# Normalized rows turned by full transposes, v's products regrouped, and identity products in planned TensorE pauses, in a window-attention and Fourier-mixer kernel

## The chip, the core and the metric

The program runs on one core of one Trainium2 chip. The metric is device time in microseconds (us) of one execution, from the first to the last instruction, with what lies around them. The core's engines are TensorE (PE in the profile, its weight loads PEld), VectorE (DVE), ScalarE (ACT), GpSimd (POOL) and SyncE (SP), which issues the DMAs here. All data is 32-bit float but the small bias product (bfloat16).

## What is computed

The input x is [8 images, 192 channels, 64 rows, 64 columns]. Two layers follow each other:

```python
# layer 0: window attention with a top-16 mask, then an MLP
shortcut = layer_norm(tokens(x))                       # over the 192 channels
q, k, v = split(windows_8x8(shortcut) @ qkv_w.T + qkv_b)   # 6 heads of 32
attn = (l2n(q) @ l2n(k).T) * temperature
attn = softmax(where(attn >= 16th_largest(attn), attn, -100) + rpb)
x2 = shortcut + unwindow((attn @ v) @ proj_w.T + proj_b)
x2 = x2 + gelu(layer_norm(x2) @ fc1_w.T + fc1_b) @ fc2_w.T + fc2_b
# layer 1: a Fourier mixer, then an MLP
y = x2 + real(ifft2(mlp_2_16_2(fft2(layer_norm(x2)))))
out = y + gelu(layer_norm(y) @ mlp1_w.T + mlp1_b) @ mlp2_w.T + mlp2_b
```

## The kernel before

**Tiling.** An image is cut into 8 bands of 512 tokens (8 rows of 64 columns, so 8 windows), and its channels into 12 groups of 16 for the Fourier part. The tasks of one image are: `front` once per band (load, transpose to tokens, norm, transpose back to channels, q, k and v), `attention` twice per band (one half of the windows each), `back` once per band (projection and MLP of layer 0), `forward`, `pointwise` (twice) and `inverse` once per channel group (the Fourier mixer; it needs all 8 bands of the image), and `leave` once per band (MLP of layer 1 and the way out; it needs all 12 groups).

**The order of work.** Nothing is ordered by hand. Every task is a Python generator that yields `op(engine, weight, mode, get, put, after)` before it emits its instructions. `issue` is a planner that runs when the program is built: it keeps a clock for each engine, in units of about 10 ns, and always emits the step that can begin first, with ties broken by due times. A step's weight is its foreseen duration; a step of TensorE costs 20 units more when its mode (the way that it tiles the array: "full", "row64", "row32", "col32", "col64", "s", "v") differs from that of the step before. `get` and `put` take and return buffers: `ps` is one of 4 PSUM tiles of [128, 2, 512], `xn` the one buffer of normalized channels, `qk` the one of q and k, `vv` one of 2 for v. A step on `EITHER` goes to ScalarE or VectorE, whichever is foreseen to end first. The engines run in the order in which the planner emits, each waiting on semaphores for its data.

**Streams.** The tasks stand in streams, each with a width (how many of its tasks are open at once) and due times in images: `front` has width 2, `attention` 4, `back` 2, `forward` 1, `pointwise` 2, `inverse` 1, `leave` 2. Image b's Fourier groups are due from b + 1.055 on, so they run beside the bands of image b + 1; in the first image there is attention and the first MLP alone.

**The part of `front` that is changed.** The normalized tokens of a band lie in `xt` (tokens on partitions, 2 x 384 columns). They go back to channels in the PSUM tile `pc`, named lc in the profile: channels 0 to 127 fill 512 columns by four PE transposes (L539, in the helper `to_channels`); channels 128 to 191 go into 256 more columns, with the window's two column halves on partitions 0 to 63 and 64 to 127. That second part is a step of its own in mode "col64": eight fp32 products of 64 columns with pieces of the identity (L680), recorded as 16 matmuls. A copy (L814, two instructions, one step on `EITHER`) reorders both parts into `xn`. Then TensorE makes the rows of q and k for the two halves of the windows (`pq`: part a over 128 channels in mode "full", L749; part b over 64 channels in "row64", L763, with the bias product L768), and of v (`pv`: part a L786, part b L798). The order of these steps is qk a(0), qk b(0), qk b(1), qk a(1), v a, v b. L809 and L810 scale `xt` on GpSimd afterwards.

Six full transposes of the same form, L539 and L544 together, are used for the MLPs' inputs already (lc_b and lc_d in the profile).

Of the kernel before, what the change touches and what calls it, by code (L numbers as in the profile page):

```python
# [15 lines left out]
C = 192  # L16
# [6 lines left out]
DFF = 768  # L23
U = 33
EPS = 1e-5
NEG = -100.0


# [1 line left out]
    return engine, weight, mode, get.split(), (put + " " + put_too).split(), after, done  # L30


def issue(streams, units):

    change = {"pe": 20, "act": 130, "dve": 0, "pool": 0}
    clock = {e: 0 for e in change}
    mode = {e: None for e in change}  # L40
    units = {name: [0] * n for name, n in units.items()}
    events = {}
    live = []

    def advance(task, value):
        try:
            found = task["gen"].send(value)
            while not isinstance(found, tuple):

                new = dict(task, gen=found, queue=None)  # L50
                live.append(new)
                advance(new, None)
                found = task["gen"].send(None)
            task["op"] = found
        except StopIteration:
            live.remove(task)
            if task["queue"] is not None:
                start(task["queue"])

    def start(queue):  # L60
        if queue[0]:
            gen, place = queue[0].pop(0)
            task = {"gen": gen, "queue": queue, "urgency": 360 * place, "last": (None, 0)}
            queue[1] += 1
            task["order"] = (queue[1], len(live), place)
            live.append(task)
            advance(task, None)

    for tasks, width in streams:
        queue = [list(tasks), 0]  # L70
        for _ in range(width):
            start(queue)
    while live:
        best, ready = {}, {}
        for task in live:
            engines, weights, kind, get, put, after, done = task["op"]
            if isinstance(engines, str):
                engines, weights = (engines,), (weights,)
            free = 0
            deps = [task["last"]] if after is None else after  # L80
            deps = [d if d[0] is None or d[0] in change else events.get(d) for d in deps]
            if any(d is None for d in deps):
                continue
            short = False
            for name in set(get):
                n = get.count(name)
                if len(units[name]) < n:
                    short = True
                    break
                free = max(free, sorted(units[name])[n - 1])  # L90
            if short:
                continue
            found = []
            for engine, weight in zip(engines, weights):
                begin = max(clock[engine], free)
                for source, end in deps:
                    if source is not None and source != engine:
                        end += 30 if source == "pe" else 15
                    begin = max(begin, end)
                new = kind and mode[engine] and kind != mode[engine]  # L100
                cost = change[engine] if new else 0
                found.append((begin + cost + weight, engine, begin, cost, task, weight))

            _, engine, *rest = min(found, key=lambda f: f[0] + 40 * (f[1] == "dve"))
            ready.setdefault(engine, []).append((engine, *rest))
        for engine, found in ready.items():
            first = min(begin + cost for _, begin, cost, *_ in found) + 15
            best[engine] = min(
                [
                    (  # L110
                        begin + cost + task["urgency"] - 100 * ("ps" in task["op"][4]),
                        task["order"],
                        f,
                    )
                    for f in found
                    for _, begin, cost, task, _ in [f]
                    if begin <= first
                ],
                key=lambda v: v[:2],
            )  # L120
        choice = min(best.values(), key=lambda v: (v[2][1], v[:2]))[2]
        engine, begin, change_cost, task, weight = choice
        _, _, kind, get, put, after, done = task["op"]
        for name in get:
            units[name].remove(min(units[name]))
        end = begin + change_cost + weight
        clock[engine] = end
        if kind:
            mode[engine] = kind
        for name in put:  # L130
            units[name].append(end + 15)
        task["last"] = (engine, end)
        if done:
            events[done] = (engine, end)
        advance(task, (engine, end))
# [3 lines left out]
def kernel(  # L139
# [25 lines left out]
        tc.tile_pool(name="psp", bufs=4, space=bass.MemoryType.PSUM)  # L165
    )

    def psum(name):
        return psp.tile([128, 2, 512], FP, tag="ps", name=name)


    ATT_BUFS, H_BUFS, XT_BUFS = 5, 7, 4
# [473 lines left out]
    def front(b, i):  # L646
# [22 lines left out]
        last = yield from normalized(xt, pair, pair, mv, f"a{nm}")  # L669
        xts[b, i] = xt  # L670

        yield op("pe", 44, "full", get="ps xn", after=last)
        pc = flat(f"lc_{nm}")
        to_channels(pc, pair, xt, parts=(0,))
        moved = yield op("pe", 43, "col64")
        side = ident.rearrange("p (e h s) -> p h e s", e=2, h=2)
        for t, j in PAIRS:
            q = 2 * t + j
            for h in range(2):
                nc.tensor.matmul(  # L680
                    pc[64 * h : 64 * h + 64, BAND + q * 64 : BAND + (q + 1) * 64],
                    xt[:, j, CA + 64 * t : CA + 64 * t + 64],
                    side[:, h],
                    start=True,
                    stop=True,
                )
        normal = yield op(EITHER, (102, 115), put="ps")
        xn = strip("xn", 1, f"xn_{nm}")
        for cols, n in ((slice(0, BAND), 8), (slice(BAND, ROW), 4)):
            copy(  # L690
                normal,
                xn[:, cols].rearrange("p (w r k) -> p r w k", w=n, k=8),
                pc[:, cols].rearrange("p (r w k) -> p r w k", w=n, k=8),
            )

        more = b == 0 and i % 2 == 1 and i < 8
        places = ("qk", "h") if more else ("qk", "vv")
# [69 lines left out]
                rows = slice(64 * t, 64 * t + 64)  # L767
                nc.tensor.matmul(pq[:, t, : 2 * C], ones3[rows], qb3[rows], start=False, **flags)  # L768

        yield op("pe", 128, "full", get=f"ps {places[0]} {places[1]}", after=[normal, "qkv"])  # L770
        pq = psum(f"pq_{nm}_0")
        qk_a(pq, 0, True)
        last = yield op("pe", 80, "row64")
# [2 lines left out]
        yield op("pe", 80, "row64", get="ps", after=[])  # L776
        pq = psum(f"pq_{nm}_1")
        qk_b(pq, 1, True)
        yield op("pe", 128, "full")
        qk_a(pq, 1, False)  # L780
        yield squares(1, pq)
        yield op("pe", 128, "full", get="ps", after=[])
        pv = psum(f"pv_{nm}")
        for p in range(2):
            for t in range(2):
                nc.tensor.matmul(  # L786
                    pv[:, t, p * C : (p + 1) * C],
                    xn[:, (2 * t + p) * 128 : (2 * t + p + 1) * 128],
                    wqkv[0][:, 2 * C :],
                    start=(p == 0),  # L790
                    stop=False,
                    skip_group_check=True,
                )
        whole = yield op("pe", 64, "row64", put="xn")
        for p in range(2):
            for t in range(2):
                rows = slice(64 * t, 64 * t + 64)
                nc.tensor.matmul(  # L798
                    pv[:, t, p * C : (p + 1) * C],
                    xn[rows, BAND + p * 128 : BAND + (p + 1) * 128],  # L800
                    wqkv[1][rows, 2 * C :],
                    start=False,
                    stop=True,
                    skip_group_check=True,
                )
        yield values(whole)

        yield op("pool", 368, after=[normal, "rows"], done=("xt", b, i))
        nc.gpsimd.tensor_tensor(xt, xt, gain1, ALU.mult)  # L809
        nc.gpsimd.tensor_tensor(xt, xt, bias1, ALU.add)  # L810

# [374 lines left out]
    def leave(b, j):  # L1186
# [40 lines left out]
    bands = [(b, i) for b in range(B) for i in range(NB)]  # L1227
    at_band = lambda b, i, late: b + i / NB + late
    groups = [(b, n) for b in range(B) for n in range(NG)]
    at_group = lambda b, n: b + 1.055 + .755 * n / NG  # L1230
    layer1 = (vec(N2G), vec(N2B))
    streams = [
        ([(setup_qkv(), -1)], 1),
# [2 lines left out]
        ([(setup_mlp(0, lambda: (wfc1, wfc2), vec(G2), vec(B2), ["rows", (None, 3000)]), -0.5)], 1),  # L1236
        ([(setup_layer1(), 0.2)], 1),
        ([(setup_mlp(1, lambda: wmlp, *layer1, ["layer1", ("att", 0, 5, 1)]), 0.2)], 1),
        ([(front(b, i), at_band(b, i, -.12)) for b, i in bands], 2),
        ([(attention(b, i, hb), at_band(b, i, -.07)) for b, i in bands for hb in range(2)], 4),  # L1240
        ([(back(b, i), at_band(b, i, .2)) for b, i in bands], 2),
        ([(forward(b, n), at_group(b, n)) for b, n in groups], 1),
        ([(pointwise(b, n, k), at_group(b, n)) for b, n in groups for k in range(2)], 2),
        ([(inverse(b, n), at_group(b, n)) for b, n in groups], 1),
        ([(leave(b, j), b + 1.69 + .55 * j / NB) for b, j in bands], 2),
    ]
    with tc.manual_schedule():
        issue(streams, units)


# [78 lines left out]
```

## Time and profile before

| | us |
|---|---|
| median of 3 runs | 4892.78 (4886.49 to 4913.86) |
| the profiled execution | 4900.75 |
| its span, first to last instruction | 4899.0 |
| VectorE busy | 2855.5 |
| ScalarE busy | 2681.7 |
| PE weight loads busy | 3656.9 |
| mean granted TensorE clock | 0.973 of full speed |

A busy time is the time in which at least one instruction of the engine is in flight. Matmuls are pipelined: each is recorded with its whole latency, so the mean duration of one is longer than the time by which it moves the next one back. What a step takes of TensorE's time is therefore read from starts: from its first start to that of the next step, less the idle time that the timeline gives between them.

### The profile page before, as it was taken

What the parts mean: (1) busy time and instruction counts of PE and PEld (TensorE: products, weight loads), DVE (VectorE), ACT (ScalarE), POOL (GpSimd) and SP (SyncE); (2) the same over time, 40 slices, a digit from 0 to 9 for tenths busy, and PEclk for the clock granted to TensorE, in tenths of its full rate; (3) what the DMA queues carried; (4) which work ended last, traced back from release to release, by engine and by line L of the source; (5) the groups of instructions that cost most, each with busy time, mean ns of one, the idle gap of its engine ahead of it and who ended that gap; (6) DMA issues with size and microseconds to landing.
All of it is one profiled execution on the core that took longest, in us unless ns stands there. A gap on an engine that the chain in (4) does not pass through costs nothing.

```text
span 4899.0 us, 145236 instructions
## 1 busy us (share of the span) xinstructions
PE 4604.9 (94%) x62794; PEld 3656.9 (75%) x62794; DVE 2855.5 (58%) x10312; ACT 2681.7 (55%) x3887; POOL 2366.7 (48%) x2195
## 2 busy tenths in 40 slices
PE   6778999999999999999999999999999999999989
PEld 4556777887778877887777877788777876778768
DVE  6877656457755467565765656665667456662111
ACT  3445656456654566544665456644666355653553
POOL 5567645355554455453655445545465354641200
PEclk7878999999999999999999999999999999999999
DMA  2000000000000000000000000000000000000000
GB/s 49 17 8 11 6 9 9 17 18 12 9 5 21 18 9 9 8 24 15 5 9 15 17 15 9 9 15 20 9 9 9 21 18 9 2 5 17 8 4 24
DMA packets 54105, 63.97 MB, mean 13 GB/s; under 512 B 17583, under 2 KB 36218, under 8 KB 53466
## 3 DMA queue, kind: packets, MB, share of 16 engines
q1 hardware_dynamic: 53454, 54.68, 3.9%
q8 instruction: 494, 8.09, 0.7%
q14 instruction: 145, 1.19, 0.1%
q10 hardware_dynamic: 12, 0.00, 0.0%
HBM read 29.29 MB, written 25.17 MB: 11 GB/s over the span
## 4 chain that ended last, share of the span: by engine, by line
PE 75%; POOL 10%; DVE 7%; ACT 5%; issue 2%; DMA 0%; SPq 0%; ACTq 0%; POOLq 0%; DVEq 0%
PE mo_d L633 10%; PE mo_b L633 9%; PE fh L1090 7%; PE mh_d L587 6%; PE mh_b L587 6%; PE fo L1117 6%; POOL nrm L733 4%; PE mh_d L600 3%; PE mh_b L600 3%; PE pq L749 3%; ACT fh L1073 2%; PE fa L1020 2%; PE fy L1165 2%; PE fb L1138 2%; PE pq L763 2%
## 5 line engine op out<-in xcount | busy, mean ns | idle before, releaser
L1073 ACT ACTIVATE fh<-fh,ab 128x1024 f32<-128x1024 f32 x768 | 815.8, 1112 | 315.9 <-PE fh L1090 313.1
L877 POOL TENSOR_TENSOR s<-s,top 128x768 f32<-128x768 f32 x128 | 191.7, 1498 | 1022.0 <-DVE s L874 613.8
L733 POOL TENSOR_TENSOR nrm<-nrm,mhalf 128x24 f32<-128x24 f32 x128 | 547.3, 4276 | 10.7
L633 PE MATMUL mo_b<-wfc,h_b 128*128 128x192 f32 x3072 | 515.9, 327 | 1.0 <-ACT fh L1073 0.7
L633 PE MATMUL mo_d<-wmlp,h_d 128*128 128x192 f32 x3072 | 513.7, 327 | 0.1
L633 PEld LDWEIGHTS mo_b<-wfc,h_b 128*128 128x128 f32 x3072 | 498.3, 190 | 9.3 <-issue 5.3
L633 PEld LDWEIGHTS mo_d<-wmlp,h_d 128*128 128x128 f32 x3072 | 498.9, 190 | 6.5 <-issue 3.0
L1090 PE MATMUL fh<-fz,w1p 32*128 32x248 f32 (+1 forms) x6144 | 458.8, 402 | 18.9 <-ACT fh L1073 9.6
L1090 PEld LDWEIGHTS fh<-fz,w1p 32*128 32x128 f32 x6144 | 289.8, 184 | 140.5 <-issue 77.2
L1117 PE MATMUL fo<-fh,w2p 128*32 128x264 f32 (+1 forms) x6144 | 382.6, 386 | 4.6 <-ACT fh L1073 3.9
L587 PE MATMUL mh_b<-hn_b,wfc_a 128*128 128x256 f32 x1536 | 379.9, 396 | 5.7 <-ACT hn_b L814 3.7
L869 DVE MAX8 top<-s 128x8 f32<-128x64 f32 x1536 | 349.8, 228 | 53.3
L587 PE MATMUL mh_d<-hn_d,wmlp_a 128*128 128x256 f32 x1536 | 367.4, 387 | 4.8 <-ACT hn_d L814 2.3
L571 ACT ACTIVATE h_d<-mh_d,fcb 128x512 f32<-128x512 f32 x384 | 240.6, 686 | 191.3 <-PE mh_d L600 149.1
L587 PEld LDWEIGHTS mh_b<-hn_b,wfc_a 128*128 128x128 f32 x1536 | 286.7, 194 | 75.3 <-issue 25.3
L867 DVE MAX8 top<-s 128x8 f32<-128x64 f32 x1536 | 319.9, 208 | 38.9 <-ACT s L814 38.6
L587 PEld LDWEIGHTS mh_d<-hn_d,wmlp_a 128*128 128x128 f32 x1536 | 285.0, 191 | 64.0 <-issue 20.9
L868 DVE MATCH_REPLACE8 s<-top,s 128x64 f32<-128x64 f32 x1536 | 320.4, 209 | 0.0
L887 POOL TENSOR_TENSOR s<-s,rsum 128x768 f32<-128x768 f32 x128 | 191.8, 1500 | 255.8 <-DVE top L867 136.8
L1117 PEld LDWEIGHTS fo<-fh,w2p 128*32 128x32 f32 x6144 | 185.5, 110 | 155.6 <-issue 32.0
L571 ACT ACTIVATE h_b<-mh_b,fcb 128x512 f32<-128x512 f32 x384 | 241.3, 688 | 108.4 <-PE mh_b L600 73.9
L1203 DVE TENSOR_TENSOR zt<-mo_d,xy 128x768 f32<-128x768 f32 x64 | 61.2, 957 | 389.2 <-PE mo_d L633 331.4
(218 smaller groups left out, 8960.7 us busy)
## 6 DMA issues: line engine op xcount, KB each, us to landing
xin<-in_x SPq DMA_DIRECT2D x64, 256.0 KB
out<-z SPq DMA_DIRECT2D x64, 256.0 KB
xin<-in_x SPq DMA_DIRECT2D x128, 64.0 KB
out<-z SPq DMA_DIRECT2D x128, 64.0 KB
wfc<-in_wfc SPq DMA_DIRECT2D x1, 576.0 KB
wmlp<-in_wmlp SPq DMA_DIRECT2D x1, 576.0 KB
wfc_a<-in_wfc SPq DMA_DIRECT2D x1, 384.0 KB
wfc_b<-in_wfc SPq DMA_DIRECT2D x2, 192.0 KB
```

Of the source, the lines that this page charges most:

```text
L571: nc.scalar.activation(h[:, k].rearrange("p (t n) -> p t n", t=2), ph[:, :, k * HALF : (k + 1) * HALF], AF.Gelu, bias=fc1_bias[:, 2 * fp + ...
L587: nc.tensor.matmul(ph[:, t, k * HALF : (k + 1) * HALF], w1[0][:, f], hn[:, t * HALF : (t + 1) * HALF], start=(first and k == 0), stop=not ...
L600: nc.tensor.matmul(ph[:, t, k * HALF : (k + 1) * HALF], w1[1][rows, f], hn[rows, BAND:ROW], start=(first and k == 0), stop=not first, skip ...
L633: nc.tensor.matmul(acc[:, j, t * C : (t + 1) * C], hs[f // 2][:, f % 2, q * 128 : (q + 1) * 128], w2[:, f, ORDER[t]], start=(f == 0 and t ...
L733: nc.gpsimd.tensor_tensor(nf, nf, mhalf[:, :24], ALU.pow)
L867: nc.vector.max(first, of)
L868: nc.vector.match_replace(s2, first, of, -3.0e38)
L869: nc.vector.max(top[:, k // 4, k % 4, 8:16], s2)
L887: nc.gpsimd.tensor_tensor(s, s, row(rsum), ALU.mult)
L1073: nc.scalar.activation(hs[hf, k], ph, AF.Gelu, bias=ab[:, 0:1])
L1090: nc.tensor.matmul(phs[k // 2][:, k % 2, cols], w1p[i][rows, hf].rearrange("p h v -> p (h v)"), fz[rows, :] if rhs is None else zu[rows, : ...
L1117: nc.tensor.matmul(po[rows, :] if i == 0 else pou[rows, :, 1 : U - 1], w2p[i][:, hf].rearrange("p a v -> p (a v)"), hs[hf, k // 2][:, k % ...
```

## The change

Four things are changed.

1. Channels 128 to 191 go back by two full transposes (L544's form) in the same step as the other four. The quarters of the 256 columns that stand on the wrong partitions are moved by the copy: it is now two steps, one instruction for the first 512 columns, and four instructions of 64 partitions x 128 elements for the rest, each step on ScalarE or VectorE.
2. v's part b comes right after qk b(1), in the run of "row64" steps; v's part a comes last.
3. The planner notes, for each TensorE step, the pause that it foresees before it and after its PSUM tiles are free. Where this is 60 units or more, `psum` emits one product of the identity with itself (128x128x128, fp32) per 22 units of pause into the new PSUM tile, ahead of the step's own products.
4. Streams: `front` is 1 wide and `attention` 3, and several due times move.

```diff
+FILL = 60
...
-def issue(streams, units):
+def issue(streams, units, lull):
...
+        if engine == "pe":
+            tiles = get.count("ps")
+            given = sorted(units["ps"])[tiles - 1] if tiles else begin
+            lull["pe"] = begin - max(clock["pe"], given)
...
+    lull = {"pe": 0}
+
     def psum(name):
-        return psp.tile([128, 2, 512], FP, tag="ps", name=name)
+        tile_ = psp.tile([128, 2, 512], FP, tag="ps", name=name)
+        pause, lull["pe"] = lull["pe"], 0
+        if pause >= FILL:
+            for _ in range(int(pause / 22)):
+                nc.tensor.matmul(tile_[:, 0, 0:128], ident, ident, start=True, stop=True)
+        return tile_
...
-        yield op("pe", 44, "full", get="ps xn", after=last)
+        moved = yield op("pe", 66, "full", get="ps xn", after=last)
         pc = flat(f"lc_{nm}")
-        to_channels(pc, pair, xt, parts=(0,))
-        moved = yield op("pe", 43, "col64")
-        side = ident.rearrange("p (e h s) -> p h e s", e=2, h=2)
-        for t, j in PAIRS:
-            q = 2 * t + j
+        to_channels(pc, pair, xt)
+        xn = strip("xn", 1, f"xn_{nm}")
+        normal = []
+        for part in range(2):
+            weights = (100, 100) if part else (62, 67)
+            normal.append((yield op(EITHER, weights, put="ps" if part else "", after=[moved])))
+            if part == 0:
+                copy(
+                    normal[0],
+                    xn[:, :BAND].rearrange("p (w r k) -> p r w k", w=8, k=8),
+                    pc[:, :BAND].rearrange("p (r w k) -> p r w k", w=8, k=8),
+                )
+                continue
             for h in range(2):
-                nc.tensor.matmul(
-                    pc[64 * h : 64 * h + 64, BAND + q * 64 : BAND + (q + 1) * 64],
-                    xt[:, j, CA + 64 * t : CA + 64 * t + 64],
-                    side[:, h],
-                    start=True,
-                    stop=True,
-                )
-        normal = yield op(EITHER, (102, 115), put="ps")
...
+                for t in range(2):
+                    copy(
+                        normal[1],
+                        xn[64 * h : 64 * h + 64, BAND:].rearrange("p (w r k) -> p r w k", w=4, k=8)[
+                            :, 4 * t : 4 * t + 4
+                        ],
+                        pc[64 * t : 64 * t + 64, BAND:ROW].rearrange(
+                            "p (r w k) -> p r w k", w=8, k=8
+                        )[:, :, 4 * h : 4 * h + 4],
+                    )
...
         pq = psum(f"pq_{nm}_1")
         qk_b(pq, 1, True)
-        yield op("pe", 128, "full")
-        qk_a(pq, 1, False)
-        yield squares(1, pq)
-        yield op("pe", 128, "full", get="ps", after=[])
+        yield op("pe", 64, "row64", get="ps", after=[])
         pv = psum(f"pv_{nm}")
...
+        yield op("pe", 128, "full", after=[])
+        qk_a(pq, 1, False)
+        yield squares(1, pq)
+        whole = yield op("pe", 128, "full", put="xn", after=[])
...
-    at_group = lambda b, n: b + 1.055 + .755 * n / NG
+    at_group = lambda b, n: b + 1.025 + .725 * n / NG
...
-        ([(front(b, i), at_band(b, i, -.12)) for b, i in bands], 2),
-        ([(attention(b, i, hb), at_band(b, i, -.07)) for b, i in bands for hb in range(2)], 4),
-        ([(back(b, i), at_band(b, i, .2)) for b, i in bands], 2),
+        ([(front(b, i), at_band(b, i, -.12)) for b, i in bands], 1),
+        ([(attention(b, i, hb), at_band(b, i, -.085)) for b, i in bands for hb in range(2)], 3),
+        ([(back(b, i), at_band(b, i, .215)) for b, i in bands], 2),
...
-        ([(leave(b, j), b + 1.69 + .55 * j / NB) for b, j in bands], 2),
+        ([(leave(b, j), b + 1.72 + .52 * j / NB) for b, j in bands], 2),
```

More of the change, by code (lines that the diff above doesn't have):

```diff
@@ L670, in front @@
         xts[b, i] = xt
-        yield op("pe", 44, "full", get="ps xn", after=last)
+        moved = yield op("pe", 66, "full", get="ps xn", after=last)
         pc = flat(f"lc_{nm}")
-        to_channels(pc, pair, xt, parts=(0,))
-        moved = yield op("pe", 43, "col64")
-        side = ident.rearrange("p (e h s) -> p h e s", e=2, h=2)
-        for t, j in PAIRS:
-            q = 2 * t + j
-            for h in range(2):
-                nc.tensor.matmul(
-                    pc[64 * h : 64 * h + 64, BAND + q * 64 : BAND + (q + 1) * 64],
-                    xt[:, j, CA + 64 * t : CA + 64 * t + 64],
-                    side[:, h],
-                    start=True,
-                    stop=True,
-                )
-        normal = yield op(EITHER, (102, 115), put="ps")
[L688 to L694, printed above, removed]
+        to_channels(pc, pair, xt)
[11 more added lines that the diff above has]
+                continue
+            for h in range(2):
+                for t in range(2):
[8 more added lines that the diff above has]
+                    )
         more = b == 0 and i % 2 == 1 and i < 8
@@ L768, in qk_b @@
                 nc.tensor.matmul(pq[:, t, : 2 * C], ones3[rows], qb3[rows], start=False, **flags)
-        yield op("pe", 128, "full", get=f"ps {places[0]} {places[1]}", after=[normal, "qkv"])
+        yield op("pe", 128, "full", get=f"ps {places[0]} {places[1]}", after=[*normal, "qkv"])
         pq = psum(f"pq_{nm}_0")
@@ L778, in front @@
         qk_b(pq, 1, True)
-        yield op("pe", 128, "full")
-        qk_a(pq, 1, False)
-        yield squares(1, pq)
-        yield op("pe", 128, "full", get="ps", after=[])
+        yield op("pe", 64, "row64", get="ps", after=[])
         pv = psum(f"pv_{nm}")
[L784 to L794, printed above, removed]
         for p in range(2):
@@ L801, in front @@
                     wqkv[1][rows, 2 * C :],
+                    start=(p == 0),
+                    stop=False,
+                    skip_group_check=True,
+                )
+        yield op("pe", 128, "full", after=[])
+        qk_a(pq, 1, False)
+        yield squares(1, pq)
+        whole = yield op("pe", 128, "full", put="xn", after=[])
+        for p in range(2):
+            for t in range(2):
+                nc.tensor.matmul(
+                    pv[:, t, p * C : (p + 1) * C],
+                    xn[:, (2 * t + p) * 128 : (2 * t + p + 1) * 128],
+                    wqkv[0][:, 2 * C :],
                     start=False,
@@ L806, in front @@
         yield values(whole)
-        yield op("pool", 368, after=[normal, "rows"], done=("xt", b, i))
+        yield op("pool", 368, after=[*normal, "rows"], done=("xt", b, i))
         nc.gpsimd.tensor_tensor(xt, xt, gain1, ALU.mult)
@@ L1244 @@
         ([(inverse(b, n), at_group(b, n)) for b, n in groups], 1),
-        ([(leave(b, j), b + 1.69 + .55 * j / NB) for b, j in bands], 2),
+        ([(leave(b, j), b + 1.72 + .52 * j / NB) for b, j in bands], 2),
     ]
     with tc.manual_schedule():
-        issue(streams, units)
+        issue(streams, units, lull)
 def _constants():
```

## The prediction

> **What bounds the kernel now.** I read the page first: shares of busy time, then the 40 slices of the span.
>
> ```profile
> PE 4604.9 (94%) x62794; PEld 3656.9 (75%) x62794; DVE 2855.5 (58%) x10312; ACT 2681.7 (55%) x3887; POOL 2366.7 (48%) x2195
> ...
> PE   6778999999999999999999999999999999999989
> ...
> PEclk7878999999999999999999999999999999999999
> ```
>
> TensorE is the bound from the fifth slice on; in the first four (the first image's attention, 490 us) nothing is full and the granted clock falls to 0.7 to 0.8. Next, the busy times of five stretches:
>
> ```profile
> 0.00:490.00 490.00, 369.08 (x4081) 286.02 (x4083) 369.47 (x1418) 215.76 (x349) 318.30 (x281) 0.82 0.09 21
> ...
> 980.00:3919.00 2939.00, 2839.62 (x39324) 2265.16 (x39322) 1787.76 (x6444) 1668.16 (x2417) 1482.85 (x1371) 0.99 0.04 13
> ...
> 4409.00:4899.00 490.00, 465.06 (x5583) 378.68 (x5581) 90.34 (x263) 219.00 (x307) 65.23 (x93) 0.99 0.05 14
> ```
>
> After the start, a microsecond taken off TensorE is nearly a microsecond of the span. At the start it is not. Third, TensorE's waits:
>
> ```profile
> PE at L894 <- POOL s L887: 92.7, 23, 14.8
> PE s L841 <- DVE qkt L831: 31.6, 15, 9.1
> ...
> PE lc_d L539 <- ACT xa_d L523: 12.4, 3, 6.0
> PE lc_b L539 <- ACT xa_b L523: 10.2, 7, 3.4
> ```
>
> Fourth, the timeline of TensorE, whole: its idle times are 282 us, of which 22 of 0.6 us or more before 490 us give 112 us (twelve of over 3.4 us: 99 us), and 80 after it give 115 us. In 2 us windows the clock costs 90 us before 490 us (the sum of one minus the clock) and 40 us after.
>
> **The full transposes.** The steps in the timeline, start, latency, line:
>
> ```profile
> 1239.37 0.66 PE L539 MATMUL lc_b<-ident,xa_b 128*128 128x128 f32 x4
> 1239.86 0.38 PE L544 MATMUL lc_b<-ident,xa_b 128*128 128x128 f32 x2
> ...
> 1244.43 0.60 PE L539 MATMUL lc<-ident,xt 128*128 128x128 f32 x4
> 1244.96 2.00 PE L600 MATMUL mh_b<-hn_b,wfc_b 64*128 64x256 f32 x16
> ...
> 1253.47 0.69 PE L680 MATMUL lc<-ident,xt 128*64 128x64 f32 x16
> 1254.09 1.15 PE L1090 MATMUL fh<-fz,w1p 32*128 32x264 f32 x16
> ```
>
> Start to start, L680 takes 0.62 us (the median of 53 steps after 490 us too) and lc's L539 0.53, together 1.15. The same six transposes as lc_b take 0.49 + 0.22 to 0.31, so 0.75 with changes of mode (about 0.1 each). Saved: 0.40 us in a band. The Trainium skill speaks against it: "TensorE: Matmul & The Clock Gate", Part 4, has a transpose at some 275 ns in context, and not counted as activity for the full clock. That would make two cost 0.55 and the saving 0.07 x 64 = 4 us. Here 275 ns is only the latency; starts are 0.11 us apart at full clock. I take the row: 0.40 x 56 bands after the first image = 22 us (range 4 to 26).
>
> **The copy.** By groups of instructions, mean ns:
>
> ```profile
> L814 ACT COPY ot<-po 128x128 f32<-128x128 f32 x111 | 30.5, 274 | 0.0
> ...
> L814 ACT COPY xn<-lc 128x512 f32<-128x512 f32 x45 | 26.4, 588 | 33.7 <-PE lc L680 33.5
> L814 ACT COPY xn<-lc 128x256 f32<-128x256 f32 x45 | 17.2, 383 | 0.0
> ```
>
> The nearest row to a 64 x 128 piece is ot's 128 x 128: four are 1.10 us for 0.38, on VectorE 4 x 0.28 for 0.41. That adds 0.7 us x 64 = 46 us to two engines with 2043 and 2217 us of idle time. As latency: 0.97 us now, 1.12 if the two steps go to two engines, 1.7 on one. TensorE's q and k wait for both copies, and behind them, in order, all of TensorE; but other tasks' steps stand between. The PSUM tile's side: lc's two TensorE steps are 4.2 us apart on average (half of the bands over 1.2 us) and become one, so lc's tile is given back earlier; pv is taken some 1.5 us earlier, so held longer. TensorE's waits for a free tile are small (releases by the Gelu L1073: some 60 us in all). I take +5 us for both (-10 to +45); without cover the copy would cost its 46.
>
> **v's products joined.** L798 takes 0.85 us start to start between other modes (the median of 52), 0.75 with one "row64" neighbour, 0.65 between two (L763 falls alike: 0.76 to 0.65). Its place is now between qk b(1) and part a: 0.65 to 0.75, so 0.10 to 0.20 less; 0.16 x 56 = 9 us (0 to 13). q and k's last squares start 0.65 us later: in the first image at most 8 x 0.65 = 5 us, on a chain that I leave to the stream term.
>
> **The identity products, warmth.** A pause costs twice: the time, and the half-rate clock behind it. I laid the chain of waits of the first 490 us on the 2 us windows: TensorE has 213 us of the chain, 43 of it at half clock (GpSimd 125, VectorE 125, whose cold stretches do not matter). Kept warm, the 43 become 21.5: 21 us saved (0 to 30). After 490 us the loss is 40 us, with TensorE nearly always on the chain. The skill's clock page (Part 1, the clock gate) asks for an idle window of about 3.4 us; only 17 of the 40 us lie behind pauses that long (3.9, 5.8, 6.0, 6.0). But the trace has the clock at 0.50 from 1164 us behind a pause of 2.2 us, and from 625 behind 1.4. By the rule, the filling is worth 17 us, by the rows up to 40. As the planner need not foresee every such pause, I take 18 (0 to 39).
>
> **The identity products, price.** The nearest row is fa's product, 132 columns: eight records, four products, take 0.90 us in a run of "full" steps, 0.225 us each. The planner's 22 units are therefore right at full clock, and about 0.45 at half. In a true pause of 0.6 us or more they cost nothing. At the very start the plan holds the first transposes to 450 units (20 products, 4.5 us warm, 9 cold; the trace waits 3.75 us there) and the bias products to 1100 (26 products; 3.5 us in the trace). I take +3 (-5 to +8), since the cold products behind get faster. Later the question is whether the foreseen pauses exist. The plan's TensorE weights of all tasks come to 4011 us, its 2215 changes of mode (counted in the timeline) to 443; the run has 4899 less 282 idle less some 65 lost by the clock, 4550. So the plan is 2% short: it sees up to 12 us an image of pauses that the run doesn't have, some 80 us over images 2 to 8 if all are long ones. These products go straight onto the path. The trace's own long pauses there are 115 us, some 1.4 us each, so most of what is foreseen has a true pause below it. I take +10 (0 to +80).
>
> **Streams.** `xn` and `qk` are single, so a second open `front` could only load and norm ahead; `sm` is 2, so of four halves only two could be in the top-16 part. Narrower streams and moved due times reorder the steps, and no row prices it: 0 (-40 to +40).
>
> **Sum.** -22 + 5 - 9 - 21 - 18 + 3 + 10 + 0 = -52 us. From the profiled execution, 4900.75, that is 4849; it stands 8.0 us over the median of the runs, 4892.78, so 4841.
>
> **The rivals.** (1) Saved time turns into waits. If the clock isn't held, because the long waits of the first image (at, s) are foreseen too short, and reordering eats a few us, only transposes and v count: -31 + 10 = -21, 4872. For it: the first image is bound by GpSimd's and VectorE's chain. Against: the waits are of 7 to 15 us, well over any threshold. (2) Slower: identity products without a pause below them, after the first image, where TensorE is full. The price is 0.22 us each. If the plan sees twice the trace's 115 us, another 115 come onto the path in place of my 10: 4841 + 105 = 4946. It decides from 76 us over my 10, some 390 products in the seven later images: then 4917 is passed. For it: the plan is 2% short. Against: an unfilled foreseen pause that had no truth would show as TensorE running late with few long waits; the trace has 80 of them. (3) The reordering takes out half of the later 115 us: 4841 - 57 = 4784.
>
> **How the numbers follow.** The likeliest, 56%: 4841, own range 4810 to 4870. Rival 1: 20%; rival 3: 15%; rival 2: 9%. A measurement of this kernel can tell 0.5%, 24 us, from no change: faster is under 4868, slower over 4917. The likeliest gives 52 of its 56 to faster, rival 3 all, rival 1 3: 0.70 faster, 0.21 same, 0.09 slower. The range takes in most of rivals 1 and 3: 4785 to 4890.
>
> **What would show it.** L680 is gone, lc has L544 with 0.11 us between starts; L798 follows L763 and takes 0.65 to 0.75. The clock in the first four slices is 9, with the page's TensorE busy near 9 there. The identity products are some 900 to 1400, over half of them before 490 us; the end of the first image comes some 20 us earlier. If TensorE's idle time after 490 us falls by more than the long waits' 115 us but the span doesn't follow, rival 2 is at work. I would be wrong if the first stretch is no shorter with the clock at full, or if the copies' 46 us appear as waits of pq on xn.

## The result, and the profile after

The change makes the kernel 1.3% faster: 4835.98 us (median of 4 runs, 4833.75 to 4839.53) against 4894.07 us, ratio 0.9874 with a 95% interval of 0.9853 to 0.9895. The profiled execution took 4839.53 us, its span 4837.7. The forecast of 4841 is met, but not by its own terms: what the identity products bring and what the new order of the work brings were each missed by some 55 us, in opposite directions. That they cancel is luck. Of one experiment (after without products and without the join) only the time is used, since its profiled execution was disturbed.

From the page of after, the lines that the prediction showed of before:

```profile
PE 4739.7 (98%) x64136; PEld 3845.5 (79%) x64136; DVE 2864.7 (59%) x10477; ACT 2653.6 (55%) x3867; POOL 2393.4 (49%) x2220
...
PE   9999999999999999999999999999999999999999
...
PEclk9999999999999999999999999999999999999999
```

TensorE is busy in every slice and the clock is full, as forecast. But 1119 of the products in it are products of the identity (2238 records, the difference between this page's x64136 and the x61898 of the run without them), and busy is not the same as useful. The busy times by stage show it. The stages are cut where the work is the same in each kernel: at the first forward transform (fa) and at the last product of v. Each line has the stretch, its length, the busy time and the instructions of PE, PEld, DVE, ACT and POOL, the granted clock, the DMA share and GB/s. After, then before:

```profile
0.00:525.00 525.00, 514.19 (x5627) 456.36 (x5628) 373.84 (x1444) 215.78 (x359) 321.64 (x284) 0.98 0.09 20
525.00:4269.00 3744.00, 3672.03 (x51978) 2928.34 (x51977) 2362.17 (x8616) 2187.24 (x3157) 1978.42 (x1816) 1.00 0.04 12
4269.00:4838.00 569.00, 553.50 (x6534) 460.79 (x6532) 128.66 (x417) 250.58 (x353) 93.38 (x122) 1.00 0.04 13
```

```profile
0.00:492.00 492.00, 371.08 (x4160) 287.60 (x4160) 371.30 (x1428) 217.50 (x354) 320.22 (x282) 0.82 0.09 21
492.00:4335.00 3843.00, 3701.78 (x52175) 2936.99 (x52174) 2355.15 (x8467) 2206.44 (x3172) 1951.90 (x1792) 0.99 0.04 12
4335.00:4899.00 564.00, 532.00 (x6463) 432.32 (x6461) 129.10 (x419) 257.78 (x363) 94.56 (x123) 0.98 0.04 13
```

So the first image became longer by 33 us, at a clock of 0.98, the middle shorter by 99, and the last Fourier groups with their way out (the tail) longer by 5. The gain lies wholly where few products were put.

The edits themselves, in TensorE's timeline of after: the six transposes, then v's part b behind the bias products.

```profile
1210.38 0.66 PE L554 MATMUL lc<-ident,xt 128*128 128x128 f32 x4
1210.87 0.38 PE L559 MATMUL lc<-ident,xt 128*128 128x128 f32 x2
1211.18 1.93 PE L1135 MATMUL fo<-fh,w2p 128*32 128x264 f32 x32
...
1246.87 0.33 PE L786 MATMUL pq<-qb,ones 64*128 64x384 bf16 x2
1247.12 0.92 PE L802 MATMUL pv<-wqkv_b,xn 64*128 64x192 f32 x8
1247.97 1.15 PE L1108 MATMUL fh<-fz,w1p 32*128 32x264 f32 x16
```

The transposes take 0.49 and 0.31 us start to start here; the medians over the bands are 0.44 and 0.31, where before had 0.53 for the four transposes and 0.62 for L680. v's part b is 0.85 us in this place and 0.75 at the median, from 0.85 before.

### The profile page after: what moved, and what is told of

The parts are those of the page before. It is cut to its first block, busy times and chain, and to the rows that moved or that the text cites. A ratio compares the mean times of both kernels' runs of the same rounds, so it can differ in the third digit from the quotient of the medians.

```text
span 4837.7 us, 147955 instructions
## 1 busy us (share of the span) xinstructions
PE 4739.7 (98%) x64136; PEld 3845.5 (79%) x64136; DVE 2864.7 (59%) x10477; ACT 2653.6 (55%) x3867; POOL 2393.4 (49%) x2220
## 4 chain that ended last, share of the span: by engine, by line
PE 82%; DVE 7%; POOL 7%; ACT 2%; issue 2%; ACTq 0%; POOLq 0%; DVEq 0%
PE mo_d L648 10%; PE mo_b L648 10%; PE mh_d L602 7%; PE mh_b L602 7%; PE fh L1108 6%; PE fo L1135 5%; PE mh_d L615 4%; PE mh_b L615 4%; PE pq L767 3%; POOL nrm L751 3%; PE fa L1038 2%; PE at L183 2%; PE fy L1183 2%; PE pq L781 2%; PE po L937 2%
## 5 line engine op out<-in xcount | busy, mean ns | idle before, releaser
L1135 PE MATMUL fo<-fh,w2p 128*32 128x264 f32 (+1 forms) x6144 | 371.4, 382 | 0.5
L602 PEld LDWEIGHTS mh_d<-hn_d,wmlp_a 128*128 128x128 f32 x1536 | 282.9, 190 | 55.2 <-issue 21.5
L905 POOL TENSOR_TENSOR s<-s,rsum 128x768 f32<-128x768 f32 x128 | 192.9, 1511 | 182.0 <-DVE top L885 113.7
L1031 POOL TENSOR_TENSOR xf<-xy,mean 128x512 f32<-128x512 f32 x96 | 108.8, 1133 | 334.3 <-PE fa L1038 334.3
```

Of the source, the lines that this page charges most:

```text
L602: nc.tensor.matmul(ph[:, t, k * HALF : (k + 1) * HALF], w1[0][:, f], hn[:, t * HALF : (t + 1) * HALF], start=(first and k == 0), stop=not ...
L905: nc.gpsimd.tensor_tensor(s, s, row(rsum), ALU.mult)
L1135: nc.tensor.matmul(po[rows, :] if i == 0 else pou[rows, :, 1 : U - 1], w2p[i][:, hf].rearrange("p a v -> p (a v)"), hs[hf, k // 2][:, k % ...
```

## The experiments

Times are set against runs of before on the same chip (4898.81, 4902.68 and 4904.19 us in the three groups). Where runs of different groups are compared with each other, the comparison goes by the ratios or by the distance of each to its own before. To compare traces I take each span apart, on TensorE: idle time by the timeline; loss by the clock while busy (the 2 us windows' shortfall, without the idle part); time of identity products from start to start; and what is left, the work at full clock.

**Without the products.** `FILL = 60` becomes `FILL = 1e9`; the order of all else is the same instruction by instruction.

> After, with FILL at 1e9: no identity product, all else kept. Theory W (the products pay by keeping the clock, and overrun the pauses of the first image): the clock in the first four slices falls back to about 0.8 and some 35 us of clock loss come back after 490 us, but the first image's end (the first forward transform, at 525 us in after) comes earlier, near 490 to 500; sum 4840 to 4870. Theory S (the streams took the waits out, the products are idle ballast): 4800 to 4830, below after, with the first image's end still late at 510 or more if the narrow streams delay it.

Measured: 4804.97 us, ratio 0.981 (0.9797 to 0.9823): the products cost 31 us. The clock does fall back to 0.81 in the first image, as W says, but W's time falls: it is below its range. The time and the late end of the first image are those of S, whose reason, the streams, is tested below. The stages of this run:

```profile
0.00:510.00 510.00, 364.25 (x3897) 283.34 (x3898) 372.36 (x1444) 216.60 (x359) 322.05 (x284) 0.81 0.08 21
510.00:4257.00 3747.00, 3661.56 (x51813) 2914.88 (x51811) 2361.60 (x8616) 2186.95 (x3157) 1977.80 (x1816) 1.00 0.04 12
4257.00:4804.00 547.00, 521.81 (x6192) 425.47 (x6190) 128.71 (x417) 250.62 (x353) 93.43 (x122) 0.99 0.04 13
```

Against after, the first image ends 15 us earlier at a cold clock, the middle is the same within 3 us, the tail is 22 us shorter. In the tail after has 41 us of products and 10 us idle, where this run has 20 us idle and 6 lost by the clock. So of the 33 us by which the first image grew, the products make 15. The other 18 are there without them: the first forward transform comes at 516 us with the transposes alone, at 508 with the join alone and at 495 with the streams alone (runs below), against 492 in before. Which wait of the first image makes it so wasn't followed.

**The products alone.** Before, with the planner's pause and `psum`'s loop of after.

> Before, with the identity products alone (same threshold and price). Theory W: the clock is 0.97 or more in every slice, 4840 to 4875; the first image's end is later than 492 us because products outlast the pauses by about 1 us each. Theory S: 4890 to 4930, the products cost as much as they save. My prediction's terms for the products sum to -26 us: 4867.

4929.89 us, ratio 1.0064 (1.0051 to 1.0077): slower by 31 us, under another order of the work, at the upper end of S's range. The stages change alike: 492 to 504, 3843 to 3838, 564 to 585. The clock is 0.996 over the whole span and the first image ends later, both as W expected, but W's time falls, and my -26 us with it.

**Why they cost.** The long pause for `at`, in after: TensorE first, then GpSimd, which makes its data (L905). Each line has start and duration in us.

```profile
270.51 12.99 PE L183 MATMUL at<-ident 128*128 128x128 f32 x114
283.34 0.82 PE L912 MATMUL at<-ident,s 128*128 128x128 f32 x6
```

```profile
280.57 1.47 POOL L905 TENSOR_TENSOR s<-s,rsum 128x768 f32<-128x768 f32 x1
282.00 0.98 POOL L750 TENSOR_SCALAR nrm<-nrm 128x24 f32<-128x24 f32 x1
```

The data is ready at 282.04; the products run until 283.34, so `at` starts 1.3 us late. This is not an exception: after the set-up, 42 of the 43 groups of products in the first image are followed by no wait at all, and the chain of waits (the work that ended last, followed back) holds 172 of the 203 us of products there. In the waits of the whole span (us in total, times, longest):

```profile
PE at L912 <- POOL s L905: 5.7, 14, 0.8
```

without the products the same wait is

```profile
PE at L912 <- POOL s L905: 93.2, 27, 11.2
```

The foreseen pauses are longer than the true ones: 203 us of products stand in the first image where the run without them idles 145 us. One reason can be read in the planner, which adds 15 to 30 units (0.15 to 0.3 us) to each handover between engines, where the chain of waits has steps of 0.02 to 0.08 us; that it is the whole reason wasn't tried. That no wait is left does not prove a loss by itself: in the middle 14 of 15 groups have none behind them either, and there the products' 21 us stand in for 14 us of idle time and 10 lost by the clock.

**Fewer, and in the first image only.** The loop takes `0.9 * pause / 22`, only for tiles of the first image's bands, and not in the set-up or the tail.

> After, with identity products only into tiles of the first image's bands (none in the set-up, none in the Fourier tail) and 0.9 of the foreseen number. Same order as after and as without products. If the overrun of about 1 us in each long pause, the set-up's products and the tail's are what the products cost, the first image ends at 490 to 500 us (510 without products, 525 in after), the tail is as long as without products, and the time is 4785 to 4800, under both. If products cost otherwise than by overrunning, 4810 to 4835.

4804.08 us, ratio 0.9802 (0.9789 to 0.9816): the same as with no product at all, and between the two forecasts. The tail's cost is gone, as expected. But the first image, expected at 490 to 500 us, ends at 511:

```profile
0.00:511.00 511.00, 470.73 (x5114) 403.66 (x5115) 373.45 (x1444) 216.43 (x359) 322.88 (x284) 0.95 0.09 21
```

The clock is 0.95, and TensorE's loss by a cold clock while busy falls from 47 to 17 us. The time doesn't follow: 31 of 36 groups after the set-up still have no wait behind them, and the chain of waits holds 22 us of products. On the same chain, TensorE's own work at half clock falls from 55 us without products to 20, worth about 17 us (an estimate: half of the difference). So warmth and overrun about cancel here; the two chains are not made of the same steps, so this is a reckoning and not a proof. Two pauses of the first image also stayed empty, as their tiles belong to the second image's first band, and the clock is 0.50 from 450 to 472 us:

```profile
448.71 1.54 PE L913 MATMUL at<-ident,s 128*128 128x128 f32 x6 [8.94 <-POOL s L906]
463.36 1.54 PE L913 MATMUL at<-ident,s 128*128 128x128 f32 x6 [11.15 <-POOL s L906]
```

What warmth alone would save, with products that always end in time, isn't shown by any run.

**The streams undone.** After, with widths 2 and 4 and the due times of before.

> After, with the widths (front 2, attention 4) and due times of before; products, transposes and join kept. Theory W: the streams are worth little, 4825 to 4850, and the first image's end stays near 525 us. Theory S: the waits after the first image come back (some 80 us idle more of TensorE than after), 4870 to 4900, and the first image's end is back near 495.

4958.38 us, ratio 1.0122 (1.0108 to 1.0136): 122 us slower than after, far beyond both theories. First image 518, middle 3851, tail 586 us. So the streams, which I had put at nothing, matter much in this company. But the number isn't theirs alone: under the old streams the planner foresees more pauses and puts in 1378 products for 1119. Of the 118 us between the spans, 62 are identity products, 47 idle time and loss by the clock, and 9 other work.

**The streams alone.**

> Before, with the widths and due times of after alone. Theory W: 4880 to 4905, as before within the order's chance. Theory S: 4830 to 4860; TensorE's idle time after the first image falls from 163 us to near 80.

4927.94 us, ratio 1.0056 (1.0043 to 1.0069): slower by 29, beyond W's range too. Idle time after the first image is 179 us against 163, so theory S falls too: narrow streams don't take waits out by themselves.

**Transposes alone, join alone, and each taken from after.** The new front (one step of transposes, two of copies) or the new place of v's part b in before; or undone in after without products.

> Before, with the full transposes and the two-step copy alone. Additive theory (each edit is worth its own TensorE work, the rest is noise): TensorE's work at full clock falls by 22 to 26 us and the time by about as much, 4870 to 4885. Order theory (the planner's order is made anew by any edit, and its waits move by tens of us either way): the work falls by the same, but the time may lie anywhere in 4840 to 4940.

> Before, with v's part b in the run of row64 steps alone. Additive theory: 4885 to 4895 (9 us less work). Order theory: work 5 to 13 us less, time anywhere in 4850 to 4945.

> After without the identity products and with the transposes undone (streams and join remain). Additive theory: 4805 + 25 = 4830. Order theory: the idle and cold time after the first image is no longer near 96 us but 130 to 210, and the time 4850 to 4930.

> After without the identity products and with the join undone (streams and transposes remain). Additive theory: 4805 + 9 = 4814. Order theory: waits anew, 4830 to 4920, at 9 us more of TensorE's work.

All runs without products, in us. The difference is to before in the run's own group. Waits are idle time and loss by the clock; work and waits add up to the span of the profiled execution.

| streams | transposes | join | time | difference | ratio to before | work | waits |
|---|---|---|---|---|---|---|---|
| old | no | no | 4899 | 0 | 1 | 4539 | 361 |
| old | yes | no | 4926 | +23 | 1.0049 | 4513 | 413 |
| old | no | yes | 4967 | +64 | 1.0130 | 4518 | 453 |
| new | no | no | 4928 | +29 | 1.0056 | 4539 | 386 |
| new | no | yes | 4858 | -45 | 0.9912 | 4518 | 333 |
| new | yes | no | 4927 | +24 | 1.0051 | not read | not read |
| new | yes | yes | 4805 | -94 | 0.9810 | 4492 | 312 |

The work adds up: the transposes take off 26 us in each pair, the join 21, the streams nothing. The times don't. The join alone costs 64 us and under the new streams saves 74; the transposes cost 23 under the old ones and save 49 on top of streams and join. The streams cost 29 alone, change nothing beside the transposes, and save 109 beside the join, with no product in the program. The additive theory falls on times. On work it holds in kind, but the join's 21 us are more than it expected. The order theory's ranges are passed too, by the join alone (4945) and by after without products and join (4920). One row is missing: old streams with transposes and join, without products, wasn't run.

**Is it the chance of the order?** The due times of all bands are moved by 0.003 images, in after without products and in before.

```diff
-    at_band = lambda b, i, late: b + i / NB + late
+    at_band = lambda b, i, late: b + i / NB + late + .003
```

> After without the identity products, with every band's due time moved by 0.003 images (about one unit of due time): the same instructions in a slightly different order. Order theory: the time moves by 10 to 60 us although no work is changed, 4815 to 4860, and the difference lies in TensorE's idle and cold time after the first image. Additive theory: 4800 to 4810.

> Before, with every band's due time moved by 0.003 images: the same instructions in another order. Order theory: 4860 to 4950, off 4899 by 10 to 50 us. Additive theory: 4890 to 4908.

4801.27 us, ratio 0.9793 (0.9779 to 0.9806), and 4908.53, ratio 1.0009 (1.0001 to 1.0017): 4 us more in before, and 4 to 9 us less without products (by the medians as they stand, or each against its own before), though the order differs from the second image on in both. For a change of order of this size my order theory, which wanted 10 to 60 us, falls. The work is not quite steady: in the nudged before it is 4528 us where before has 4539, with the same instructions, so some 10 us of the table's work can be order. The long waits are steadier: TensorE's waits of 1 us or more in the middle stage are 48 (80 us) in before and 49 (97 us) in the nudged one, 19 (27 us) in after without products and 20 (29 us) nudged. Streams and join without the transposes have 36 (56 us). So the three edits together do take waits out, and one small nudge does not bring them back; larger changes of the order with the same instructions weren't tried. By what mechanism the waits go stays open.

**The transposes at a fixed order.** After without products, its plan kept, but L680's eight products in the place of the two transposes, and one copy in the place of four.

> After without the identity products, with the plan and the order kept step for step, but the second part of the way back made by the eight col64 products of before in the place of the two transposes (in the same step), and copied by one instruction in the place of four. This prices the transposes at a fixed order. By the trace's rows: 0.40 us more of TensorE in a band, 22 to 26 us in all, less a few for the shorter copy: 4805 + 22 = 4827. If the transposes were no cheaper than the 275 ns that the Trainium skill states, 4805 to 4810. If the four small copies had been on the path, under 4805.

4816.36 us, ratio 0.9825 (0.9812 to 0.9839), short of the 4827 expected. The work is 4514 us, 22 more than without products, as the rows said; of it 6 us (each against its own before) to 11 (by the medians as they stand) reach the end, and the intervals of the two ratios overlap. In the middle the work is 17 us more and the stage 9 longer, since idle time and loss by the clock are 8 us less. Nothing here puts the small copies on the path.

## Why the prediction was right, and where it was not

Its number came out by compensation, which is luck. Its own sign of being wrong came true: the first stretch is no shorter, but 33 us longer, with the clock at 0.98. By its own steps:

- **The full transposes** were right in size: 1.15 us to 0.75 a band, 26 us of work (22 after the first image). The 275 ns a transpose of the Trainium skill's "TensorE: Matmul & The Clock Gate", Part 4, were rightly left aside for the row: at a fixed order the work differs by 22 us, not by 4. Whether transposes count as activity for the clock, which that part denies, no run here shows. But "a microsecond taken off TensorE is nearly a microsecond of the span" looks too strong: at a fixed order a quarter to a half of the 22 us came through, as far as the noise lets one say.
- **The copy** cost what the rows said, and stayed off the path. In after, by groups:

```profile
L832 ACT COPY xn<-lc 128x512 f32<-128x512 f32 x63 | 37.1, 590 | 42.6 <-PE lc L559 42.6
L832 ACT COPY xn<-lc 64x128 f32<-64x128 f32 x84 | 22.0, 262 | 1.0 <-DVE xn L832 0.2
...
L832 DVE COPY xn<-lc 64x128 f32<-64x128 f32 x172 | 49.6, 288 | 111.7 <-ACT xn L832 109.9
```

  262 and 288 ns stand against the 274 and 280 forecast, and the two parts mostly go to two engines: the first to ScalarE in 63 of 64 bands, the second to VectorE in 43. TensorE's waits have no line of pq on xn.
- **The join** did in its own steps what was forecast, 9 us. By starts at full clock after the first image, the steps of q, k and v of one band take 6.91 us in before and 6.80 with the join alone, 6.94 and 6.81 in the pair under the new streams: 7 to 9 us over 64 bands. The other 12 to 14 of the 21 us of work lie in steps of other tasks (those of fh fall by 9 to 12 us), which have other neighbours in the new order. Why is open: the timeline has 139 changes of mode less with the join alone, but only 45 less in the pair under the new streams, for the same 21 us.
- **The products' price** is the step that failed: "In a true pause of 0.6 us or more they cost nothing." They are longer than the pauses: 15 us net in the first image by overrunning, and 22 in the tail, where 41 us of products met 26 us of idle and cold time. In the middle, where I feared up to 80 us, the plan sees few pauses: 21 us of products, at no cost. Two readings behind that fear were a little off: before has 2255 changes of mode in its trace, not 2215, and loses 78 us by the clock while busy, not 65, so the plan is 1.7% short instead of 2.
- **The products' warmth** brought no saving that a run shows: "Kept warm, the 43 become 21.5: 21 us saved". Two thirds of the cold loss in the first image were removed with the fewer products, and it ended at 511 us instead of 510. By the chain of waits some 17 us may have been saved there and lost again to overrunning. The terms for the products sum to -26 us; the measurement is +31, in two orders of the work.
- **The streams** at 0 (-40 to +40) were the other failure: +29 alone, within the range, but -109 beside the join, far outside. That edits of the order don't add was in no term. Streams, transposes and join together take 49 us of waits out (361 to 312), beside 47 us of work. My own third rival, reordering that takes half of the later waits out, came true together with part of the second, products without a true pause; the likeliest case as I worked it out did not.

The version without products beats both kernels: 0.981 of before, where after has 0.9874, and the intervals do not meet.

## What to carry to other kernels

Filling a pause is free where the filling ends before the data comes: look behind each filled pause for a remaining wait, and where there is none, ask whether the filling is on the chain of waits. The same kernel without the filling is the cheapest test, and here it was the faster one. In a kernel whose order a planner makes, work and waits of an edit should be measured apart: here the work added up to within some 10 us, the waits didn't, and an edit tried alone (+23, +29 and +64 us) says little of what the three do together (-94).

## What the runs showed of the hardware

The granted clock can fall behind short pauses: in before it is 0.50 from 3041 us behind a pause of 1.4 us, from 2874 behind one of 1.7 and from 2594 behind one of 2.1. In after the filled pauses keep it at 0.98 over the first image, where it was 0.82. A step of v's part b takes 0.85 us between steps of other modes and 0.75 with one neighbour of its own mode, so a change of the array's mode costs about 0.1 us of TensorE there. An fp32 product of 128 x 128 x 128 takes about 0.22 us at full clock (114 records, 57 products, in 12.8 us).
